# A depthwise 3x3 convolution on TensorE: sixteen 32x32 diagonal tiles in place of one 128x128 diagonal

## The chip, the cores and the metric

The kernel runs on one core of one Trainium2 chip, in one launch. The metric is the time on the device in microseconds; before the change it is 35,322.73 us, the median of three runs (35,309.54 to 35,332.95). One profiled execution stands behind every other number here. Its span is 35,280.6 us.

The core has a matrix engine (TensorE, PE in the profile, with its weight loads on a row of their own, PEld), a vector engine (VectorE, DVE), a scalar engine (ScalarE, ACT), a general engine (GpSimd, POOL) and a queue that issues most transfers (SyncE, SP). TensorE writes its results to PSUM[...]. The other engines bring results from PSUM to the on-chip memory SBUF.

## The reference

The input is one image of 256 x 256 positions with 128 channels, in float32. Two layers follow each other, each with a residual. The first is row attention. The second is a selective scan in four directions, ahead of which a depthwise 3x3 convolution stands. Cut to what matters here:

```python
# layer 1, on the group-normed image (65,536 positions of 128 channels)
xz = x @ w_in.T                      # 128 -> 512
xi, z = jnp.split(xz, 2, axis=-1)    # 256 channels each
z = silu(z)
xc = conv3x3(xi, conv_w, groups=256, padding="SAME") + conv_b
xc = silu(xc)                        # every channel has its own nine weights
...                                  # projections, scan, norm, times z, w_out
```

Every channel is convolved by itself: output channel d at a position is the sum over nine neighbours of that channel times nine weights of d.

## The kernel before, in words

The kernel runs in stages. First come the statistics of the first group norm, then the attention over 32 blocks of eight rows, then the convolution stage, and last the scan with 512 steps, which fills the larger part of the span. Between the stages the data lies in the chip's main memory: `x2_d` (the image after attention, a token to a row), `xc_d` (the convolution's output, a token to a row of 256), `z_d` (channel by channel).

The convolution stage is the block from line 382 to line 493. Its order on each engine is decided by a scheduler, which looks at priorities and dependencies and may move instructions; the scan stands in an order written out by hand (`manual_schedule`, line 944), which is not touched.

A strip holds 16 image rows (`RS`), and there are 16 strips. The tile `xi` (line 412) has 18 rows of 258 columns, with the channels on the partitions and the two halves of 128 channels (`h`) side by side. GpSimd clears the border columns (lines 413 and 414) and copies the last two rows of the strip before it (line 420).

To fill a strip, the loop of line 425 takes two image rows (512 tokens) at a time:

- `xbd` (line 429): a load of 512 tokens from `x2_d`, four buffers.
- `tpd` (line 433): four transposes on TensorE, to bring channels onto partitions.
- `xn` (line 436): VectorE subtracts the mean and multiplies by the reciprocal deviation.
- `pxi` (line 442): a 128x128 by 128x512 matmul for each half; VectorE copies it into `xi` (line 446).
- `pz` (line 452): the same for the gate; ScalarE applies silu into `zt` (line 460), which is stored to `z_d` (line 461). `pxi` and `pz` share two banks (tag `pj`).

To convolve, the loop of line 465 takes two output rows (a pair) at a time, eight pairs to a strip, and both halves. For each of the nine taps TensorE multiplies a 128x128 matrix, whose diagonal holds the tap's weights of the 128 channels (`diag`, line 389), by a shifted window of `xi` of two rows by 256 columns. The nine products accumulate in one bank (`pc`, line 468, two buffers). ScalarE adds the bias and applies silu into `xcs` (line 478), four transposes bring it back to tokens on partitions (`pt`, line 485), VectorE copies that into `xct` (line 488), and a store goes to `xc_d` (line 490). A float32 matmul of the program is recorded as two matmul instructions, with a weight load each, so 128 pairs x 2 halves x 9 taps give 4608 records.

Three lines outside this stage appear below, since they show how TensorE treats parts of its array. Line 749 sums over states: matmuls of 128 rows by 32 columns (`yp`), four of them writing four groups of 32 partitions. Line 298 gives attention scores (`sc`) from 64-row operands, whose two heads lie on partitions 0 to 63 and 64 to 127. Lines 589 and 771 are transposes and a matmul of the scan.

## Time and profile before

| What | Value |
|---|---|
| Time, median of three | 35,322.73 us |
| Span of the profiled execution | 35,280.6 us |
| Convolution stage | 4325.7 to 7001.2 us |
| TensorE busy in 4334 to 7001 us | 2664.50 us |
| of it pc, as a union | 2031.5 us |
| pxi and pz, as unions | 245.7 and 252.2 us |
| pt and tpd, as unions | 168.0 and 67.5 us |
| One pc matmul record | 592 ns |
| One copy xi<-pxi, xct<-pt (VectorE) | 688 and 692 ns |
| One xcs (ScalarE) | 687 ns |
| Moved by the DMA engines in the stage | 166.81 MB, 63 GB/s |

A record of a matmul lasts from the start of its reading to a modelled end, and records overlap; the distance from start to start is what a matmul costs in a dense stream. Unions count overlapping time once. A row of a group gives, after the bar, the busy time as a union, the mean length of one record, then the idle time of the engine just ahead of such instructions and what ended it. In a windows row, the busy time of each engine in the stretch is followed by the number of its instructions; PEclk is the share of TensorE's full clock that was granted; the last two numbers are the mean busy share of the 16 DMA engines and the rate. A wait row reads: who waited, for whom, the microseconds in total, the times, and the longest.

### The profile page before, as it was taken

The numbers are of one execution on the slowest core, as the hardware profiler recorded it, in microseconds if no ns is written. First come the engines' busy times: TensorE is split into PE (matmuls) and PEld (weight loads), VectorE is DVE, ScalarE is ACT, GpSimd is POOL, SyncE is SP. The second block draws the span as 40 slices with busy tenths as digits, with TensorE's granted clock in tenths as the row PEclk, the third lists the DMA queues.
The fourth block names the chain that finished last, engine by engine and source line by source line (L and its number), as shares of the span: only waits on it lengthen the run. The fifth ranks groups of instructions, "written<-read, shape, count | busy, mean of one in ns | idle before, by whom it ended". The sixth has DMA issues, their size and how long they took to land.

```text
span 35280.6 us, 352910 instructions
## 1 busy us (share of the span) xinstructions
PE 26226.3 (74%) x109078; PEld 12390.7 (35%) x109078; DVE 29738.4 (84%) x29211; ACT 25019.2 (71%) x50182; POOL 25808.4 (73%) x11291
## 2 busy tenths in 40 slices
PE   5999899967677777777777777777777777777776
PEld 2555544433333333333333333333333333333333
DVE  7666611199999999999999999999999888888888
ACT  3555411188888788888888888888888777777777
POOL 4222200088888888888888888888888888888888
PEclk8999999977777777777777777777777777777777
DMA  3000111144444444444444444444444444444444
GB/s 128 29 29 29 32 62 62 65 104 104 106 104 105 103 105 107 115 114 116 114 115 115 117 115 115 116 114 116 115 116 115 112 109 112 110 109 111 110 111 102
DMA packets 2099611, 3516.78 MB, mean 100 GB/s; under 512 B 201384, under 2 KB 1187368, under 8 KB 2022832
## 3 DMA queue, kind: packets, MB, share of 16 engines
q1 hardware_dynamic: 2094832, 3492.87, 39.3%
q8 instruction: 857, 14.04, 0.2%
q14 instruction: 1042, 8.54, 0.1%
q10 hardware_dynamic: 2880, 1.34, 0.0%
HBM read 2754.17 MB, written 739.25 MB: 99 GB/s over the span
## 4 chain that ended last, share of the span: by engine, by line
POOL 49%; PE 23%; issue 11%; ACT 8%; DVE 8%; POOLq 0%; DMA 0%; ACTq 0%; DVEq 0%; SPq 0%
POOL bx L1026 34%; PE pc L471 6%; POOL du L662 3%; POOL delta L659 3%; PE yp L749 3%; DVE bx L1009 3%; POOL lg L656 2%; PE ur L723 2%; ACT dA L983 2%; DVE bx L734 2%; PE av L341 2%; POOL at L318 2%; POOL hst L1025 1%; ACT bt L693 1%; PE atp L330 1%
## 5 line engine op out<-in xcount | busy, mean ns | idle before, releaser
L1026 POOL TENSOR_TENSOR bx<-bx,C_r 128x2048 f32<-128x2048 f32 x4096 | 18602.6, 4542 | 334.0 <-POOL hst L1025 6.8
L1009 DVE TENSOR_TENSOR_SCAN bx<-dA,hst,bx 128x512 f32<-128x512 f32 x12192 | 15105.8, 1266 | 1234.0 <-ACT dA L983 1234.0
L723 PE MATMUL ur<-du,spread 128*128 128x512 f32 x8192 | 6490.3, 886 | 4357.5 <-DVE bx L734 4357.5
L983 ACT ACTIVATE dA<-dr,A_s 128x512 f32<-128x512 f32 x12288 | 8364.9, 686 | 1484.8 <-DVE bx L1009 1450.7
L734 DVE TENSOR_TENSOR bx<-B_r,ur 128x1536 f32<-128x1536 f32 x4096 | 7080.4, 1729 | 35.7 <-PE ur L723 35.7
L693 ACT ACTIVATE bt<-duT,B_t 128x128 f32<-128x128 f32 x16384 | 5664.6, 399 | 0.0
L1009 DVE TENSOR_TENSOR_SCAN bx<-dAl,hst,bl 128x512 f32<-128x512 f32 x4064 | 5116.1, 1259 | 576.5 <-ACT dAl L983 262.5
L749 PE MATMUL yp<-bx,gather 128*32 128x512 f32 x32768 | 4605.6, 690 | 12.3 <-POOL bx L1026 12.2
L705 PE MATMUL bl<-ident,bt 128*128 128x128 f32 x16384 | 3349.7, 340 | 1233.1 <-DVE bx L1009 1232.8
L705 PEld LDWEIGHTS bl<-ident,bt 128*128 128x128 f32 x16384 | 2317.8, 172 | 3379.3 <-DVE bx L1009 2623.5
L723 PEld LDWEIGHTS ur<-du,spread 128*128 128x128 f32 x8192 | 1695.1, 257 | 4988.9 <-DVE bx L734 4988.8
L1025 POOL COPY hst<-bx 128x4 f32<-128x4 f32 x4096 | 770.0, 188 | 3029.8 <-DVE bx L1009 2872.5
L983 ACT ACTIVATE dAl<-dr,A_s 128x512 f32<-128x512 f32 x4096 | 2936.7, 717 | 0.0
L318 POOL TENSOR_TENSOR at<-at,sm 128x2048 f32<-128x2048 f32 x256 | 922.3, 3603 | 2707.7 <-DVE sm L317 2568.4
L749 PEld LDWEIGHTS yp<-bx,gather 128*32 128x32 f32 x32768 | 1379.9, 126 | 3755.6 <-issue 3459.8
L675 PE MATMUL tpd<-ident,du 128*128 128x128 f32 x4096 | 979.3, 417 | 1842.7 <-POOL du L662 1842.7
L471 PE MATMUL pc<-xi,diag 128*128 128x512 f32 x4608 | 2031.5, 592 | 0.0
L488 DVE COPY xct<-pt 128x512 f32<-128x512 f32 x256 | 177.1, 692 | 1837.8 <-PE pt L487 1837.8
L616 PE MATMUL pv<-bc,dtw_s 8*128 8x512 f32 x2048 | 1201.8, 713 | 629.3 <-ACT bc L605 629.3
L681 ACT COPY duT<-tpd 128x512 f32<-128x512 f32 x1024 | 600.4, 586 | 1478.8 <-PE tpd L675 1478.8
L675 PEld LDWEIGHTS tpd<-ident,du 128*128 128x128 f32 x4096 | 775.0, 217 | 2474.0 <-POOL du L662 2474.0
L922 ACT COPY yo<-yp 128x512 f32<-128x512 f32 x1024 | 597.1, 583 | 1470.0 <-PE yp L749 1469.6
(166 smaller groups left out, 35061.1 us busy)
## 6 DMA issues: line engine op xcount, KB each, us to landing
dr<-de_d SPq DMA_DIRECT2D x4096, 256.0 KB
C_r<-bc_d SPq DMA_DIRECT2D x2048, 256.0 KB
B_r<-bc_d SPq DMA_DIRECT2D x2048, 192.0 KB
de_d<-delta SPq DMA_DIRECT2D x512, 512.0 KB
xtok<-xc_d SPq DMA_DIRECT2D x256, 512.0 KB
xtok<-xc_d SPq DMA_DIRECT2D x512, 256.0 KB
yl<-y_d SPq DMA_DIRECT2D x512, 256.0 KB
y_d<-yt SPq DMA_DIRECT2D x512, 256.0 KB
```

What stands on the lines that cost most here:

```text
L318: nc.gpsimd.tensor_tensor(at, at, sm.unsqueeze(3).to_broadcast([P, H, 2, S]), ALU.mult,)
L471: nc.tensor.matmul(pc, diag[:, h, t, :], xi[:, h, 2 * q + dy : 2 * q + dy + 2, dx : dx + S], start=(t == 0), stop=(t == 8),)
L616: nc.tensor.matmul(pv, dtw_s[:, k, h * P : (h + 1) * P], bc[:R, :], start=True, stop=True)
L675: nc.tensor.transpose(tp[:, b, h * P : (h + 1) * P], prepared[q][2][:, h, t0 : t0 + P], ident)
L693: nc.scalar.mul(bt[:, b, :, j, :], duT[:, b, h * P : (h + 1) * P].rearrange("t (g c) -> t g c", c=32), B_t[:, b, n : n + 1],)
L705: nc.tensor.transpose(bl[:, b * P : (b + 1) * P], bt[:, b, g % 4].rearrange("t j c -> t (j c)"), ident)
L723: nc.tensor.matmul(ur, spread[:, g % 4].rearrange("p j c -> p (j c)"), prepared[q][2][:, g // 4, :], start=True, stop=True,)
L734: nc.vector.tensor_tensor(bx[:, :NB, :], prepared[q][3], ur.unsqueeze(1).to_broadcast([P, NB, T]), ALU.mult,)
L749: nc.tensor.matmul(yp[32 * g : 32 * g + 32, :], gather, hc[:, i, :], start=(i == 0 and steps[q][0] != ORDER[0]), stop=True, skip_group_che ...
L983: nc.scalar.activation(dA, dr, AF.Exp, scale=A_s[:, k, g // 4, g % 4, i : i + 1])
L1009: nc.vector.tensor_tensor_scan(hs[:, i, :], dA, hs[:, i, :] if i < NB else bls.pop((q, g)), 0.0 if a == 0 else hst[:, g, i : i + 1], ALU.mult,
L1026: nc.gpsimd.tensor_tensor(hs, hs, prepared[q][4], ALU.mult)
```

## The change

The convolution uses the array as sixteen tiles of 32x32. A diagonal 128x128 matrix has non-zero entries only in its four 32x32 diagonal blocks; so 32 channels need only a 32x32 diagonal. The change cuts the 128 channels of a half into four groups `r` of 32 partitions and takes four pairs of rows `c` (eight image rows, a block) at once. Tile (r, c) of the array takes channel group r of row pair c: it reads the partitions 32r to 32r+31 of `xi`, at the rows of pair c, and writes the partitions 32c to 32c+31 of bank `pc{r}`. Sixteen matmuls make a tap, and four banks hold a block's half, each with four row pairs below each other and one channel group.

What follows from it: the bias tile `cb_s` is laid out by (c, r); `diag` shrinks to 32 columns; the transposes back turn a bank with four pairs, and the copy to `xct` puts 32 channels of four pairs in place; `xct` now holds eight rows and is stored in one piece. `pc` takes four banks with one buffer each, and `pt` shares the two banks of the tag `tr` with `tpd`. `xbd` has ten buffers in place of four, `xcs` eight, `xn` three.

The stage is also put in program order by hand. In each half of a block it convolves, transposes the next rows' tokens (`turn_rows`), and then takes turns between the transposes back of the previous half (`back`) and the projections of the next block's rows (`project`). Loads are issued two blocks ahead.

```diff
-        cb_s = cw.tile([P, 2], F32, name="cb_s")
-        nc.scalar.dma_start(cb_s, conv_b)
-        diag = cw.tile([P, 2, 9, P], F32, name="diag")
+        cb_s = cw.tile([P, 2, 4], F32, name="cb_s")
+        for c in range(4):
+            for r in range(4):
+                nc.scalar.dma_start(
+                    cb_s[32 * c : 32 * c + 32, :, r], conv_b[32 * r : 32 * r + 32, :]
+                )
...
+        diag = cw.tile([P, 2, 9, 32], F32, name="diag")
...
-            for q in range(RS // 2):
-                xct = cs.tile([P, 4, DI], F32, name="xct")
-                for h in range(2):
-                    pc = cp.tile([P, 2, S], F32, name="pc", tag="pc")
-                    for t in range(9):
-                        dy, dx = divmod(t, 3)
+        def convolve(k, h):
+            xi = strips[k * RB // RS]
+            e = k * RB % RS
+            pcs = [cp.tile([P, 512], F32, name=f"pc{r}", bufs=1) for r in range(4)]
+            for t in range(9):
+                dy, dx = divmod(t, 3)
+                for c in range(4):
+                    for r in range(4):
+                        rp = slice(32 * r, 32 * r + 32)
+                        e0 = e + 2 * c + dy
                         nc.tensor.matmul(
-                            pc,
-                            diag[:, h, t, :],
-                            xi[:, h, 2 * q + dy : 2 * q + dy + 2, dx : dx + S],
+                            pcs[r][32 * c : 32 * c + 32, :],
+                            diag[rp, h, t, :],
+                            xi[rp, h, e0 : e0 + 2, dx : dx + S],
                             start=(t == 0),
                             stop=(t == 8),
+                            skip_group_check=True,
                         )
+            xcs = []
+            for r, pc in enumerate(pcs):
+                x_ = cs.tile([P, 512], F32, name="xcs", bufs=8)
+                nc.scalar.activation(x_, pc, AF.Silu, bias=cb_s[:, h, r : r + 1])
+                xcs.append(x_)
+            return xcs
...
+        with tc.manual_schedule():
+            xbs = {u: load_rows(*u) for k in range(2) for u in units_of(k)}
+            strip(0)
+            for r, nr in units_of(0):
+                turns(project(0, r, nr, turn_rows(nr, xbs.pop((r, nr)))))
+            behind = []
+            for k in range(NBK):
+                ahead = units_of(k + 1) if k + 1 < NBK else []
+                if k + 2 < NBK:
+                    xbs.update({u: load_rows(*u) for u in units_of(k + 2)})
+                xct = cs.tile([P, 4, 4, DI], F32, name="xct")
+                for h in range(2):
+                    xcs = convolve(k, h)
+                    if h == 0 and ahead and (k + 1) * RB % RS == 0:
+                        strip((k + 1) * RB // RS)
+                    mine = [
+                        (r, nr, turn_rows(nr, xbs.pop((r, nr)))) for r, nr in ahead[2 * h : 2 * h + 2]
+                    ]
+                    turns(
+                        *behind,
+                        (p for r, nr, xn in mine for p in project(k + 1, r, nr, xn)),
+                    )
+                    behind = [back(k, h, xct, xcs)]
+            turns(*behind)
```

`units_of(k)` lists the two-row units of block k; `turns` steps through its generators one piece at a time, one of each in turn.

## The prediction

> **What bounds the kernel now.** I read the strip of the span in 40 slices first, to find the stage, then the answer by windows for that stage, the chain of waits inside it, and the tile answer for pc. The convolution stage runs from 4325.7 us (first transpose of xbd after the statistics) to 7001.2 us (end of the last copy into xct): 2675.5 us, 7.6% of the span. Its windows row:

> ```profile
> core 0: us, PE busy (x) PEld busy (x) DVE busy (x) ACT busy (x) POOL busy (x), PEclk, DMA share, GB/s
> 4334.00:7001.00 2667.00, 2664.50 (x7156) 1168.69 (x7153) 449.79 (x640) 331.81 (x518) 19.41 (x44) 1.00 0.18 63
> ```

> TensorE is busy for 2664.5 of 2667 us at a granted clock of 1.00; VectorE has 17%, ScalarE 12%, the DMA engines 18%. A busy TensorE is not always the bound, so the chain over 5000 to 6800 us is the check:

> ```profile
> by line: PE pc L471 73.8%; PE pz L453 9.4%; PE pxi L443 8.7%; PE pt L487 6.0%; PE tpd L435 1.7%; ACT xcs L479 0.4%; issue 0.1%; ACTq L479 0.0%
> ...
> 5040.85 7.73 PE pc L471 x18
> ```

> The chain stays on TensorE, three quarters of it on pc. Eighteen matmul instructions (nine taps, each recorded as two) take 7.73 us: 0.4294 us each, 0.859 us per 512-column tap. All 4608 give 1979 us; the remaining 696 us are projections, transposes and small waits. The other engines wait for this line:

> ```profile
> ACT xcs L479 <- PE pc L471: 1898.6, 256, 7.7
> DVE xct L488 <- PE pt L487: 1837.8, 256, 7.7
> ```

> So anything taken from pc comes straight off the span, until another engine or a wait takes over.

> [...] No row of this kernel has sixteen, but two have parts of it. yp (L749) uses four column tiles:

> ```profile
> L749 PE MATMUL yp<-bx,gather 128*32 128x512 f32 x32768 | 4605.6, 690 | 12.3 <-POOL bx L1026 12.2
> ```

> 32768 instructions of 690 ns cover only 4605.6 us, 141 ns each. In a timeline at full clock (from 20019.6 us) four of them start in every 0.43 us, so four columns run abreast in float32, each with its own moving data. Two row tiles also overlap:

> ```profile
> 2510.26 1.33 PE L298 MATMUL sc<-qT,kT 64*128 64x256 f32 x8
> ```

> Eight sc instructions, each 0.214 us apart from the next on its own rows, start within 0.95 us; one after another they would need 1.71. Four rows times four columns is an extension of both. [...] sixteen tiles need 32 matmuls and 32 weight loads per 0.859 us, 27 ns per pair. [...] the semaphore instructions of the TensorE queue at L589 and L771 are 125 ns apart in 231 of 382 cases; one takes 51 ns and four transposes (eight instructions) stand between, so at most (125-51)/8 = 9 ns each. [...] After yp the next 128-wide matmul starts at 20022.82 us, before the modelled end of yp at 20022.89: a drain of tenths of a microsecond, no more.

> **The change, part by part.**
> - Removed: 4608 instructions x 0.4294 = 1979 us.
> - Added: 32 blocks of eight rows x 2 halves x 9 taps = 576 taps of sixteen matmuls. If the sixteen run abreast, a tap costs what one matmul costs, 0.859 us: 576 x 0.859 = 495 us. If only four do (what yp shows), it costs 3.435 us and 1979 us again. I take the first, because row tiles overlap in sc, [...]and the four row tiles write four different banks; both ends are kept below.
> - Start skew, tail and two mode changes per half: estimate 0.5 us (matmul tail 0.592 - 0.429 = 0.16; the rest from the drain above), so a half's convolution is 9 x 0.859 + 0.5 = 8.2 us.
> - Between two convolutions stand two units of two rows: 8 transposes at (1.04 - 0.27)/7 = 0.11 us, 16 transposes back of the previous half at 0.11, 8 projection matmuls at 0.859: 0.9 + 1.8 + 6.9 = 9.5 us of TensorE. Waits: the first transposes back need the tr buffer that xn frees: 0.44 (four transposes) + 0.2 + 0.81 (xn) = 1.5 us after the start, when TensorE has done 0.9: 0.6 us lost. Afterwards VectorE (copies of 0.69) stays less than a buffer behind, as the transposes back stand between the projections; I add 0.2 for the last pj turns. Sum 10.3 us. ScalarE's four xcs (4 x 0.687 = 2.7 us) run beside the transposes, before the first pz ends at about 5.5 us, so the four single pc banks are free 7 us before the next convolution asks.
> - VectorE per half: 2 x 0.81 + 8 x 0.69 = 7.1 of 18.5 us. DMA: the same 166 MB that took a share of 0.18 in 2667 us need about 0.4 in 1200. The xi halo copy (1.04 us on GpSimd, 15 times), strip memsets and 16 small cb_s loads lie beside TensorE work.
> - TensorE's instruction fetch: 57 fetches for 14,309 instructions here, about 256 each, at 0.1% of 16 engines, some 1 us apiece; the new stage needs one per 3.4 us. Hidden.
> - Program order: 62 halves with units x (8.2 + 10.3) = 1147 us. Ahead of them five units alone, each a chain of transposes 0.44, xn 1.0, four matmuls 3.4 and turns 0.4, about 24 us in all (one is half size). After them two halves without units, 2 x (8.2 + 3) + 4 = 26 us. Stage: 1197 us.
> - Added around it: the last store is four times larger before the scan can read it, and ScalarE issues 15 more loads ahead of the first pz: estimate 20 us for both.
> - The scan's instructions stand in the same order on every engine: no change.

> Sum: -2675.5 + 1197 + 20 = -1458; 35,323 - 1458 = 33,865, rounded to **33,870**.

> **The rivals.**
> 1. The 128-wide part waits on evacuation: if each of the four transpose groups waits for its own copy (0.69 + 0.15), 3.4 us per half, 62 x 3.4 = +211: **34,080**. For it: two banks each for tr and pj. Against it: VectorE is under 40% busy and interleaved.
> 2. Only eight tiles run abreast (two rows per column, the widest row overlap in this trace): a tap is 1.718, +495: **34,365**. [...]
> 3. The weight loads do not overlap: 32 loads per tap at yp's 110 ns shown one by one, 3.52 us, so 576 x 3.52 = 2028 in place of 495: **35,400**, slower. Against it: in yp eight loads start within 50 ns; but those were four columns of the same rows.
> 4. VectorE or DMA as the bound: needs 2.5 times the 7.1 us or the 0.4 share; no separate time.

> **How the numbers follow.** Forecast 0.72; rival 1 0.11; rival 2 0.10; rival 3 0.07. The forecast and rival 1 hold 0.83, so the range runs from dense TensorE work (64 x (7.7 + 9.5) = 1101 plus 24 and 20, some 33,790) to 34,200, above rival 1 with room for a tap of 1.0 us. Faster: the first three, less a little for something between 2 and 3, 0.92; same 0.01; slower 0.07.

> **What would show it.** The changed profile should have 18,432 pc matmuls of near 592 ns whose union is 500 to 540 us; about 18.5 us from one convolution to the next; a granted clock of 1.00; a stage near 1200 us still on TensorE in the chain, with pz and pxi (8 x 0.859 = 6.9 of 18.5 us) nearly as large as pc. Rival 1 shows as TensorE idle before pt or pxi, released by VectorE; rival 2 as a convolution of 15.5 us with pairs of starts; rival 3 as pc starts spaced 110 ns. A scan that changed its length would make the whole account wrong.

## The result, and the profile after

The changed kernel takes 34,014.58 us (median of four, 34,002.76 to 34,029.72) against 35,326.21 us before on the same chip: a ratio of 0.963, 95% interval 0.9615 to 0.9646. It was forecast at 33,870 us with a range of 33,790 to 34,200. The direction held, and so did the mechanism (sixteen tiles run at once), but the forecast was 145 us too low: of the 1453 us that it promised, 1312 came.

The convolution stage now runs from 4320.4 to 5694.4 us: 1374.0 us in place of 2675.5. The rest of the span hardly moved (28,279.4 us after the stage before, 28,306.6 in this profile and 28,276.4 in a second profile of the same kernel). The windows row of the stage, in the columns of the one shown for before:

```profile
4320.00:5694.50 1374.50, 1305.50 (x21001) 684.80 (x21000) 440.66 (x650) 312.43 (x518) 19.39 (x44) 1.00 0.37 121
```

TensorE is still the busy engine and the granted clock is still 1.00. VectorE and ScalarE do the same work in half the time, and the DMA share doubled to 0.37. The chain of waits from 4400 to 5500 us:

```profile
by line: PE pc L511 47.6%; PE pz L486 17.2%; PE pxi L475 16.6%; PE pt L531 9.2%; DVE xn L463 3.8%; issue 2.9%; PE tpd L461 2.8%
...
4557.65 10.48 PE pc L511 x268
```

pc is now 47.6% of the chain in place of 73.8%. But the last row is not what was forecast: a half's convolution takes about 10 us, not 8.2. The tile answer for pc (after the count: the shortest, median and longest record in ns, then the first and last start) and its windows row in the stage (PE, PEld and ACT) give the size:

```profile
L511 PE MATMUL pc<-xi,diag x18432: 584/587/613, 4347.0 to 5687.5; 32*32 32x512 f32 x199
```

```profile
4320.00:5694.50 1374.50, 654.45 (x18432) 353.89 (x18432) 155.13 (x256) 1.00 0.37 121
```

18,432 records of 587 ns, as forecast, cover 654 us, not 500 to 540. Sixteen tiles do run at once: in the trace the sixteen first matmuls of a convolution start within 0.10 us. The excess is between the taps and in holes. A timeline shows one hole; the numbers ahead of the engine are the start and the length, and the bracket is the idle time ahead:

```profile
4834.55 5.55 PE L511 MATMUL pc<-xi,diag 32*32 32x512 f32 x165
...
4835.44 0.55 PEld L511 LDWEIGHTS pc<-xi,diag 32*32 32x32 f32 x32 [0.33 <-issue]
4836.29 3.08 PEld L511 LDWEIGHTS pc<-xi,diag 32*32 32x32 f32 x100 [0.31 <-issue]
4841.84 0.24 PEld L511 LDWEIGHTS pc<-xi,diag 32*32 32x32 f32 x32 [2.47 <-issue]
4841.84 4.42 PE L511 MATMUL pc<-xi,diag 32*32 32x512 f32 x123 [1.74 <-issue]
```

In the middle of a convolution nothing starts for 2.3 us, and no engine is named: "issue" is time in which the engine waited for nothing that the profile shows. Then 32 weight loads come at once.

I took the stage apart by starts in the trace, over 62 halves. From the first pc to the next transpose: 10.66 us on average, 9.68 at the least. From there to the next pc: 10.58 us. The start with five units alone: 26.6 us. Against the forecast that is 64 x (10.66 - 8.2) = 157 us, 62 x (10.58 - 10.3) = 17 us and 3 us, together the 177 us by which the stage is longer. The 10.66 us have two parts. A tap comes 1.045 us after the one before it (median of all), where the array needs 0.859. And the difference of 0.98 us between mean and shortest is the holes, 63 us in 64 halves; the ten shortest convolutions, 9.68 us each, have none.

So the questions were: why does a tap cost 1.045 us, what makes the holes, and which half of the change, tiles or order, brings the gain?

### The profile page after: what moved, and what is told of

Same layout as the page of the kernel before. It is cut to its first block, busy times and chain, and to the rows that moved or that the text cites. A ratio compares the mean times of both kernels' runs of the same rounds, so it can differ in the third digit from the quotient of the medians.

```text
span 34001.0 us, 379815 instructions
## 1 busy us (share of the span) xinstructions
PE 24860.1 (73%) x122902; PEld 11865.3 (35%) x122902; DVE 29725.8 (87%) x29214; ACT 25003.3 (74%) x50182; POOL 25821.5 (76%) x11291
## 4 chain that ended last, share of the span: by engine, by line
POOL 51%; PE 20%; issue 12%; DVE 8%; ACT 8%; POOLq 0%; DMA 0%; SPq 0%; DVEq 0%; ACTq 0%
POOL bx L1110 35%; POOL du L746 4%; POOL delta L743 3%; PE yp L833 3%; DVE bx L1093 3%; POOL lg L740 3%; PE ur L807 2%; DVE bx L818 2%; ACT dA L1067 2%; PE pc L511 2%; PE av L341 2%; POOL at L318 2%; POOL hst L1109 2%; PE atp L330 1%; POOL e L734 1%
## 5 line engine op out<-in xcount | busy, mean ns | idle before, releaser
L310 ACT ACTIVATE at<-at,mx 128x256 f32<-128x256 f32 x2048 | 1016.0, 498 | 472.0 <-DVE mx L306 467.3
L734 POOL TENSOR_TENSOR e<-e,du 128x1024 f32<-128x1024 f32 x512 | 1208.3, 2360 | 138.2 <-ACT du L730 138.2
```

What stands on the lines that cost most here:

```text
L734: nc.gpsimd.tensor_tensor(e, e, du, ALU.subtract)
```

## The experiments

### Which half of the change brings the gain

**The order alone.** One 128x128 diagonal per row pair, as before, in the new order:

```diff
-            for t in range(9):
-                dy, dx = divmod(t, 3)
-                for c in range(4):
-                    for r in range(4):
...
+            for c, pc in enumerate(pcs):
+                for t in range(9):
+                    dy, dx = divmod(t, 3)
+                    e0 = e + 2 * c + dy
+                    nc.tensor.matmul(
+                        pc,
+                        diag[:, h, t, :],
+                        xi[:, h, e0 : e0 + 2, dx : dx + S],
+                        start=(t == 0),
+                        stop=(t == 8),
+                    )
...
```

`diag`, the bias tile and the transposes back (left out above) go back to the old layout with it.

> The new program order alone: the stage in the hand-written order with its buffers, but each row pair convolved with one 128x128 diagonal, as before the change. If the tiles carry the gain: a half takes 4 x 7.73 + about 10.5 us, 64 of them 2650 us, less two halves without projections and plus a start of some 25 us, so the stage is about as long as before and the time is 35,290 to 35,340. Rival: the order carries a part of the gain by itself (waits of the old order removed): 100 us or more below 35,326.

Measured: 35,267.85 us against 35,274.51, ratio 0.9998 (0.999 to 1.0007). The order brings nothing by itself; TensorE was busy without gaps before (2664.5 of 2667 us). The four row pairs of a half stand together in the chain, at 0.859 us per tap as before:

```profile
4390.06 30.91 PE pc L501 x72
```

**The tiles alone.** The changed kernel without its hand-written order:

```diff
-        with tc.manual_schedule():
+        if True:
```

> The sixteen tiles without the hand-written order: the same code, but the scheduler decides. It puts one lone matmul of the next convolution between the transposes and the projections of each half, so two more changes between tiled and whole use of the array, and a lone tile for 0.86 us. If changes of mode and lone matmuls cost what they seem to (about 1 to 1.5 us per half): 60 to 100 us more than the unaltered kernel beside it. Rival: the lone matmul fills the wait for xn, and the time is within 20 us of it.

Measured: 33,992.92 us (33,985 to 33,998) against 33,980.83 (33,976 to 33,985) for the unaltered kernel beside it: 12 us more, within the 20 us of the rival. The lone matmul does not add its 0.86 us in full, and the chain of this run shows why:

```profile
by line: PE pc L511 50.9%; PE pz L486 16.8%; PE pxi L475 16.3%; PE pt L531 8.7%; PE tpd L461 4.7%; issue 2.6%
```

`DVE xn`, 3.8% of the changed kernel's chain, is gone: the lone matmul stands where TensorE waited for xn (in one half it starts at 4808.77 us, behind the transposes of the next rows, and the transposes back follow at 4809.75). The tiles carry the gain, all but some 12 of 1300 us.

### Why a tap costs more than the array needs

The first idea came from the numbers: 64 instructions in 1.073 us (the period I read off one convolution first) are 16.8 ns each, which looked like a rate at which the queue hands on instructions. The second: weight loads go in only between one matmul instruction and the next. Both were guesses. Three kernels were to tell them apart.

**Half the columns.**

```diff
-                            pcs[r][32 * c : 32 * c + 32, :],
+                            pcs[r][32 * c : 32 * c + 32, :S],
                             diag[rp, h, t, :],
-                            xi[rp, h, e0 : e0 + 2, dx : dx + S],
+                            xi[rp, h, e0, dx : dx + S],
...
```

The second row of each pair is left out; ScalarE reads the 256 columns twice, so that its work stays the same.

> Each of the sixteen matmuls of a tap takes 256 columns in place of 512: it computes the first row of each pair only, and that row is written for both. The count of instructions stays the same. In the changed kernel a tap of 64 instructions (32 matmuls, 32 weight loads) comes every 1.073 us where the array alone would need 0.859. Theory D (the queue hands on one instruction every 16.8 ns, so 64 of them take 1.07 us): a tap stays at 1.07 us, a convolution without holes at about 9.2 us from first to last start, the time within 30 us of the changed kernel's 34,015. Theory L (weight loads go in only between passes of the moving data, which costs half a matmul instruction per tap): a tap falls to 2.5 x 0.216 = 0.54 us, and the time falls by up to 64 x 9 x 0.53 = 305 us, to about 33,710. Theory F (beside either of them, at every 256th instruction of the queue the array waits for instructions to be fetched, up to 2.3 us): under L the holes grow, since 256 instructions are used up in 2.2 us, and give back 100 to 200 us of it.

Measured: 33,910.88 us against 35,274.51 on this chip (ratio 0.9613, interval 0.9599 to 0.9628), so 1364 us less where the changed kernel has about 1300. The median tap is 0.63 us. That ends theory D: with the same 64 instructions a tap may be shorter than 1.07 us. It does not fit L either (0.54). Both medians, 1.045 and 0.63, are two instructions' start-to-start time plus about 0.2 us: 2 x 0.429 + 0.19, and 2 x 0.215 + 0.20. A constant is lost per tap. It is about the tail of a recorded matmul, 0.587 - 0.429 = 0.158 us, and 0.03. Taps that are 0.41 us shorter are worth some 240 us, and only 70 came, against 33,980.83 us for the changed kernel on this chip. The holes, which come back below, took most of the rest. And the granted clock, 1.00 in the changed kernel's stage, is 0.95 in this one:

```profile
4346.00:5626.00 1280.00, 1085.46 (x20918) 625.41 (x20918) 425.93 (x621) 302.62 (x504) 19.38 (x44) 0.95 0.39 128
```

**Another order within the tap.**

```diff
-                for c in range(4):
-                    for r in range(4):
+                for r in range(4):
+                    for c in range(4):
```

> Only the order of the sixteen matmuls of a tap changes: channel group (row tile) in the outer loop, row pair (column tile) in the inner. Theory D: nothing that counts changes, a tap stays at 1.07 us and the time within 20 us of 34,015. Theory L: which load meets which pass changes; if loads of one column group are what collides, a tap falls towards 0.86 us and the time by up to 576 x 0.21 = 120 us, to 33,890; if loads of one row group collide, it rises. Theory F: the holes stay where they are in the count of instructions (every 256th), about 60 us in all.

Measured: 33,980.19 us (ratio 0.9632, 0.9616 to 0.9648) against 33,980.83 for the unaltered kernel on this chip, median tap 1.045 us. Nothing changed. In these two orders at least, it does not matter which load meets which row or column group.

**Eight tiles at a time.**

```diff
-            for t in range(9):
-                dy, dx = divmod(t, 3)
-                for c in range(4):
+            for t in range(18):
+                dy, dx = divmod(t % 9, 3)
+                for c in range(t // 9 * 2, t // 9 * 2 + 2):
...
```

> The same sixteen tiles and instructions, but in program order first row pairs 0 and 1 for all nine taps, then pairs 2 and 3: eight tiles run at once, 32 instructions per half tap. Theory D (16.8 ns per instruction): 32 instructions need 0.54 us, less than the array's 0.859, so a half tap takes 0.859 us without a stall, a convolution 18 x 0.859 = 15.5 us, and the time is 34,015 + 64 x (15.6 - 10.3) = about 34,355. Theory L (half an instruction is lost per round of weight loads): 1.073 us per half tap, 19.3 us, about 34,600. Theory F: 256 instructions last 6.9 us or more, so the holes at every 256th instruction shrink to nearly nothing in both.

Measured: 34,255.78 us (ratio 0.9711, interval 0.9696 to 0.9725), slower than sixteen, as it must be with twice the rounds, but with no stall at all: 15.02 us from the first pc to the next transpose, in every half. That ends theory L, which had 19.3. The rows of TensorE and its weight loads in one convolution:

```profile
4627.28 15.09 PE L511 MATMUL pc<-xi,diag 32*32 32x512 f32 x288
```

```profile
4628.17 0.15 PEld L511 LDWEIGHTS pc<-xi,diag 32*32 32x32 f32 x8 [0.28 <-issue]
4628.60 0.15 PEld L511 LDWEIGHTS pc<-xi,diag 32*32 32x32 f32 x8 [0.28 <-issue]
4629.03 0.15 PEld L511 LDWEIGHTS pc<-xi,diag 32*32 32x32 f32 x8 [0.28 <-issue]
```

Eight weight loads every 0.43 us: each round of matmuls starts when the array is free, with the next weights loaded behind it. In the changed kernel, starts in the trace show something else: of the next tap's weight loads only the first few come while the present tap runs, and some 28 come in one burst, which begins 0.03 us after the second matmul of one of the present tap's first tiles has ended.

**Twelve tiles.** A test at 48 instructions per round:

```diff
-            for t in range(9):
-                dy, dx = divmod(t, 3)
-                for c in range(4):
+            for t in range(18):
+                dy, dx = divmod(t % 9, 3)
+                for c in (0, 1, 2) if t < 9 else (3,):
...
```

> Row pairs 0, 1 and 2 first for all nine taps (twelve tiles, 48 instructions per round), then pair 3 alone (four tiles). Theory W ([...]sixteen tiles need 64 instructions per tap, so the next tap's loads come in only after the tap's second instruction has ended: 0.43 + 0.59 + 0.03 = 1.045 us, as measured, and 0.215 + 0.374 + 0.03 = 0.62 us with 256 columns, where 0.63 was measured): 48 instructions leave room for the next tap's, so a round of twelve takes 0.859 us. The stalls seen with sixteen are then gone, and a convolution takes 2 x 9 x 0.859 less some overlap, about 15.2 us. Rival P (the array or its memories slow down in proportion to the tiles at work, 12/16 of the extra 0.186 us): a round of twelve takes 0.95 to 1.0 us. Either way slower than the changed kernel, by about 64 x 4.5 = 290 us.

Measured: 34,309.64 us against 33,980.83, so 329 us more; a convolution takes 15.8 us on average and 15.35 without holes (15.2 expected). In the rounds of twelve the starts repeat every 0.859 us (for one convolution 2.386, 3.245, 4.104, 4.964 us after its first). No part of the stall is left at twelve. That speaks against a slowing in proportion to the tiles at work, and for a limit that 48 instructions per round do not meet and 64 do.

**One instruction per matmul.** Sixteen tiles, but half the instructions:

```diff
-        diag = cw.tile([P, 2, 9, 32], F32, name="diag")
+        diag = cw.tile([P, 2, 9, 32], BF16, name="diag")
...
-            xi = cs.tile([P, 2, RS + 2, W], F32, name="xi")
+            xi = cs.tile([P, 2, RS + 2, W], BF16, name="xi")
```

> The changed kernel with xi and diag held in bfloat16[...]: a matmul of the program is then one instruction with one weight load in place of two with two, so 32 instructions per tap[...]. Theory W[...] a round of two taps takes 0.215 + 0.373 + 0.03 = 0.62 us, a tap 0.31 us, above the array's 0.215; a convolution takes about 3.0 us in place of 10.7, and the time falls by 64 x 7.7 = 490 us, to about 33,490 to 33,530. If the drain per tap had another cause than the count of instructions (sixteen tiles writing the same four banks again): 0.215 + 0.19 = 0.40 us per tap, 3.9 us per convolution, about 33,560. Theory F: 288 instructions per convolution, with 9 us of other work between, leave few holes at every 256th.

Measured: 33,476.75 us against 35,279.54 (ratio 0.9489, interval 0.9473 to 0.9504). A tap takes 0.218 us, a quarter of 0.859, against the 0.215 taken for the array without a stall. That ends the alternative, 0.40 us per tap because sixteen tiles write the same four banks again. (The data's type changes here together with the count of instructions; sixteen float32 tiles with half the instructions were not run.) But my 0.31 us for theory W was wrong, and by its own rule: I let the count move in steps of two taps, where the rule counts instruction by instruction. The matmul that stands 64 instructions on is two taps away and is wanted 0.43 us later; by the rule it may go in after 0.37 + 0.03 us. So it is never late. The same reckoning gives no stall at twelve tiles (64 instructions are 1.33 rounds, 1.15 us, against 1.05) and one at sixteen (0.86 against 1.05). With that theory W fits all five cases. It remains my explanation. What the runs show is narrower: float32 rounds of 32 and 48 instructions have no stall, those of 64 have one, and with 32 bfloat16 instructions for the same sixteen tiles it is gone. As every matmul here has one load, a limit of 32 matmuls would fit as well as one of 64 instructions.

### What makes the holes

I counted TensorE's records (loads, matmuls and the queue's semaphore instructions) up to each gap of more than 0.45 us within a convolution (0.7 us in half columns). In the changed kernel there are 40, 56 us in all, and every one stands at the same count modulo 256, namely 193. That count comes up 144 times within convolutions, so 104 times nothing happens there. A half has 656 records, not a multiple of 256, so a wait that the program itself causes would not return at one count. With half the columns there are 73 holes, all at 193, 197 us in all. With twelve tiles there are 15, with eight none. With bfloat16, where the count comes up 73 times, there are nine, again all at 193: 16.7 us, four of them above 3 us. 256 is also what one packet of the instruction queue brings, by that queue's row for the stage, with its packets, megabytes and share:

```profile
q8 instruction: 164, 2.69, 0.8%
```

2.69 MB over 164 packets are 16.4 KB each, and the 42,001 records of TensorE in the stage are 164 times 256. So I take a packet for the fetch of a block of 256 instructions. It takes 0.96 us (the median of the 164), but 38 of the 40 holes end 2.2 to 2.5 us after the packet before them began. A block lasts 256/64 x 1.045 = 4.2 us with sixteen tiles and 2.5 us with half columns, so there the holes multiply; it lasts 6.9 us with eight, and they vanish. That is not the whole rule: with bfloat16 a block lasts 1.7 us within a convolution, which is hardly longer than one block, and the holes are few but long. Why a fetch that takes 2.4 us is late at all when a block lasts 4.2 us, and why it is late in some places only, the runs leave open.

### A version that is faster than both

TensorE idles after each convolution of the changed kernel, since the first transposes back need a bank that xn has to free:

```profile
4804.55 0.66 PE L531 MATMUL pt<-ident,xcs 128*128 128x128 f32 x4 [0.47 <-DVE xn L463]
```

The transposes of the next rows can go ahead of the convolution:

```diff
+                    mine = [
+                        (r, nr, turn_rows(nr, xbs.pop((r, nr)))) for r, nr in ahead[2 * h : 2 * h + 2]
+                    ]
                     xcs = convolve(k, h)
...
-                    mine = [
-                        (r, nr, turn_rows(nr, xbs.pop((r, nr)))) for r, nr in ahead[2 * h : 2 * h + 2]
-                    ]
```

> The changed kernel itself, unaltered, as the measure for the three beside it on this chip: 33,960 to 34,020 us, depending on the chip.

> In each half the eight transposes of the next rows are put ahead of the convolution in place of after it, so that VectorE makes xn while the convolution runs and the first transposes back find their banks free. In the changed kernel TensorE is idle 0.47 us there and 0.3 us more around it, in each of 62 halves. If that wait is real: 25 to 50 us less than the unaltered kernel beside it. If it only moves elsewhere (VectorE gets to the copies earlier, and the last pj banks bind): within 15 us of it.

Measured: the unaltered kernel 33,980.83 us (ratio 0.9631, 0.9616 to 0.9645), the altered one 33,926.24 (0.9615, 0.9601 to 0.963). The runs of the two do not overlap (33,922 to 33,935 and 33,976 to 33,985): 55 us less. In the timeline the transposes back now follow the convolution at once:

```profile
4799.40 7.45 PE L511 MATMUL pc<-xi,diag 32*32 32x512 f32 x212
4806.78 0.66 PE L531 MATMUL pt<-ident,xcs 128*128 128x128 f32 x4
...
4815.75 1.04 PE L461 MATMUL tpd<-ident,xbd 128*128 128x128 f32 x8
```

The 128-wide part fell from 10.58 to 9.88 us, 43 us in 62 halves. So the wait was real. The convolution fell too, from 10.71 to 10.45 us, some 16 us in all, as 25 holes remained of 41. That part was not foreseen and takes the gain above the 25 to 50 us expected; why the holes became fewer, no run shows.

## Why the prediction was right, and where it was short

- **What bounds.** TensorE without gaps, three quarters of it pc: right. The order alone moved nothing, and what pc lost came off the span.
- **Sixteen abreast.** Right: all start within 0.10 us, and rivals 2 and 3 did not happen. The yp and sc rows were a fair base. One reading of yp was off: of its first eight weight loads six start within 50 ns, and the other two 0.28 us later.
- **The tap.** This is the term that was mis-sized. "If the sixteen run abreast, a tap costs what one matmul costs, 0.859 us" measured 1.045 us. The step looked at whether the array could run sixteen and at how fast instructions are handed on, and not at how many a round has. yp, the model, has 16 instructions per round of four tiles; here 48 ran without a stall and 64 did not. Together with the start and the tail a hole-free convolution is 9.68 us in place of 8.2: 95 us.
- **Instruction fetch: "Hidden".** Wrong, 63 us. The fetch was priced at some 1 us from the share of its queue; from its beginning to the next instruction are 2.2 to 2.5 us, and in a stage where 656 instructions run per half it shows.
- **Hand-on rate, at most 9 ns.** Right, and generous: 32 loads and 16 matmuls start within 0.13 us, 2.7 ns each. The first matmuls of different tiles start 6.7 ns apart.
- **The 128-wide part.** 10.58 us against 10.3; rival 1 (each group waits for its copy) would have been 13.7.
- **DMA, ScalarE, banks.** Right: a share of 0.37, and the four single banks are waited for 0.2 us in the whole stage.
- **The surroundings.** The 20 us allowed for the last store and the small loads are not confirmed: the part after the stage is 27 us longer than before in the first profile of the changed kernel and 3 us shorter in the second, and in the eight other runs between 6 us shorter and 7 us longer. No run shows why the first one differs.
- **The range.** The time lies in it, in part by luck. Its upper end was drawn above rival 1, which did not happen. The room for a tap of 1.0 us did what it was meant for, since taps of 1.045 us add 107 us; the holes came on top of it.

## What to carry to other kernels

Cutting the array into small tiles multiplies the instructions per round. Count them, loads included, and twice for float32, which this trace records as two loads and two matmuls. On this kernel 48 per round (twelve tiles) ran without a stall, 0.859 us, and 64 (sixteen tiles) took 1.045 us, though sixteen still did more per microsecond. When an engine is idle for "issue" in mid-stream, count instructions to the gap. Here all 40 holes stood at one remainder modulo 256, the number of instructions to a packet, in a loop of 656 instructions, and that pointed to the fetch and not to a dependency.

## What was not expected of the hardware

- A stream of sixteen float32 tiles loses 0.19 us per tap, a constant that does not shrink with the columns (0.20 with half of them); with one instruction per matmul it is gone (0.218 us per tap of sixteen tiles).
- TensorE stalls within convolutions at one place in 256 instructions, and not each time: at 40 of 144 such places in the changed kernel, up to 2.4 us, and at 73 with half the columns, up to 4.4 us. With eight tiles, where a block lasts 6.9 us, there is no such hole.
- With half the columns some long holes are followed by a lower clock. It is 0.50 in 33 stretches of the stage, 137 us in all, and each of them begins within 4.5 us of the end of an idle stretch of TensorE of 1.9 us or more (not every such idle stretch has one). In the changed kernel, where the longest idle stretch is 1.8 us, the clock stays at 1.00. One of the 33, behind a hole of 4 us:

```profile
4490.00:4494.40 4.40, 3.85 (x122) 2.87 (x123) 0.00 (x0) 0.00 (x0) 0.00 (x0) 0.50 0.04 11
```
